# Layer 1's experts in pairs of tiles from tile 13 on, with larger portions in the late edge blocks

## The chip, the core and the metric

The kernel runs on one core of one Trainium2 chip. The metric is the device time of one execution in microseconds; times of several executions are given by their median. The engines are named as the profile names them: PE is the matrix engine, PEld its weight loads, DVE the vector engine, ACT the scalar engine, POOL the engine that issues the indirect gathers, SP the engine whose queue issues most plain transfers.

## The reference, cut to what matters

The program is a two-layer graph network on 3125 nodes of 256 values and 100000 edges, sorted by destination. Layer 0 (two mean-aggregation steps, a linear attention, a mixture of 8 experts) is untouched. The change is in layer 1, which computes

```python
xn = _layernorm(x, axis=-1)
x = x + _L1_gnn_ref(xn, ...) + _L1_mix_ref(xn[None], ...)[0]
x = x + _L1_ffn_ref(_layernorm(x, axis=-1)[None], ...)[0]
...
h1 = relu(einsum('bsd,edh->bseh', features, expert_w1) + expert_b1)
h2 = relu(einsum('bseh,ehf->bsef', h1, expert_w2) + expert_b2)
expert_out = einsum('bsef,efo->bseo', h2, expert_w3) + expert_b3
```

`_L1_gnn_ref` is a graph attention over the edges (a softmax over the edges of each destination, then a weighted sum of source rows). `_L1_ffn_ref` computes all six experts of three 256x256 layers for every node, and mixes the best two by a router. A node's experts can start only when all its incoming edges have been summed.

## The kernel before, in words

The nodes lie in 25 tiles of 128 (`NB = 25`), and the running sum of layer 1 is `xs[:, t, :]`. Layer 1 is the class `Layer1`, and the order of its instructions on PE, DVE and ACT is written out by hand (`manual_schedule`): what an engine gets first it runs first.

**Edge blocks.** The edges are cut into `NK = 31` blocks: block 0, blocks 1 to 29 of 28 columns of 128 edges, and the small block 30. `run` walks over them. For block b it first issues the gathers of block b+1 (`gather`, L1592: one indirect transfer per column on POOL, into the tiles `r0`, 16 columns, with three buffers, and `r1`, 12 columns, with two), and then calls `block(b)`, which on PE, DVE and ACT computes scores, a running maximum, exponentials, the messages (L1700, DVE) and their sums by destination (L1706, PE, tile `sums`). The sums of block b-1 are divided and placed into `xs` inside block b (`close`, `place` L1762, `placed` L1770). When the last block that touches a node tile has been placed, the tile is closed: `settle`, `deviation`, `normed` and `turned` (L1813, L1815) normalise it and put its transpose into the tile `xt`. At most one tile is closed in a block, except in the last `LASTS = 4` blocks, 27 to 30, where `whole` places the block's own sums at once and closes all that is ready.

**Expert groups.** `TOGETHER` lists which neighbouring tiles share one pass of the experts, as (first tile, number of tiles). When `turned` has transposed the last tile of a group, it appends `group(t0, nt, xt)` to `self.queue`. `group` is a generator. Between its `yield`s it issues units: one expert layer half (`layer`, L1447: four matmuls over all the group's columns, 256 for a pair and 384 for three tiles, then an activation, L1450), a result for up to two tiles (`result`, L1516: eight matmuls; its addition into `xs`, L1522, is held back in `self.late`), the router (L1439, L1462 and a chain of small DVE operations, L1464 to L1505), and a bias step (L1533 to L1541). It also issues the weight loads on SP (`weights`, 256 KB each, 18 per group, tile names `ew1` to `ew3` with two buffers each, L358). At most one group runs at a time.

**The planner.** Each `yield` names the unit's cost in the planner's own units, called credits here: `1.8 * nt / 4` for a layer half, 0.9 per tile for a result. `take(x)` adds x to `self.credit` and issues units until the credit is used up; when no group is queued the credit is set to zero, and the place stays empty. `block` calls `take` at eleven places: four before the exponentials with 2, 2, 1 and 2 credits, and seven between the message pieces that share 12; so a block takes 19 credits, times `PORTION.get(b, 1.0)`. `whole` takes 2 + 2 more, and 1 + 1 for each tile it closes. What is left after the last block is issued by `take(1e9)`.

**Other queues around it.** `places(b+2)`, at the end of block b, issues four loads `a<-apart` (L1349) on SP, behind any weight load that still waits for its buffer; their consumer is the matmul L1388 of the next block. `store` issues finished output tiles on SP.

The lines that the change touches are these constants:

```python
942  GB = 3
943  TOGETHER = [(0, 2), (2, 2), (4, 3), (7, 3), (10, 3), (13, 3), (16, 2), (18, 2), (20, 2), (22, 1), (23, 2)]
944  LASTS = 4
945  PORTION = {NK - 6: 1.2, NK - 5: 1.2, NK - 4: 1.2, NK - 3: 1.2, NK - 2: 1.0, NK - 1: 0.5}
```

and the lines that use them:

```python
1605         more = PORTION.get(b, 1.0)
1606         takes = [x * more for x in (2, 2, 1, 2, 12, 0)] if self.keyed else KEYING
...
1807         t0, nt = next(g for g in TOGETHER if g[0] <= b < g[0] + g[1])
```

(in line 1807, b is the tile that is being closed.)

Of the kernel before, what the change touches and what calls it, by code (L numbers as in the profile page):

```python
# [915 lines left out]
NK = len(BQ)  # L916
# [23 lines left out]
WHOLE = [[t for t in range(NB) if max(b for b in range(NK) if t in TILES[b]) == k] for k in range(NK)]  # L940
CW = QC
GB = 3
TOGETHER = [(0, 2), (2, 2), (4, 3), (7, 3), (10, 3), (13, 3), (16, 2), (18, 2), (20, 2), (22, 1), (23, 2)]
LASTS = 4
PORTION = {NK - 6: 1.2, NK - 5: 1.2, NK - 4: 1.2, NK - 3: 1.2, NK - 2: 1.0, NK - 1: 0.5}
KEYING = (3.2, 3.2, 0, 3.2, 0, 1.6)
GROUPS1 = GROUPS[:5] + [(2560, 256), (2816, 256), (3072, 128)]
TS = 256
# [356 lines left out]
class Layer1:  # L1305
# [293 lines left out]
    def block(self, b, part, A, N):  # L1599
# [4 lines left out]
        mk, m4 = A["mk"], A["m4"]  # L1604
        more = PORTION.get(b, 1.0)
        takes = [x * more for x in (2, 2, 1, 2, 12, 0)] if self.keyed else KEYING
# [195 lines left out]
    def turned(self):  # L1802
# [3 lines left out]
        nc = self.nc  # L1806
        t0, nt = next(g for g in TOGETHER if g[0] <= b < g[0] + g[1])
        g = b - t0
# [1178 lines left out]
```

## Time and profile before

| what | value |
|---|---|
| four runs | 3466.73, 3452.87, 3470.64, 3467.14 us |
| their median | 3466.94 us |
| the profiled execution's own time | 3462.25 us |
| its span, first to last instruction | 3460.2 us |
| mean granted clock of PE | 0.812 |
| PE busy | 2360.6 us (68%), 11819 matmuls |
| DVE busy | 1682.6 us (49%) |
| ACT busy | 896.8 us (26%) |
| POOL busy | 1039.3 us (30%) |
| gathers `r` on POOL | 826, 949 ns each at the median, from 1637.6 to 3300.8 us |

Layer 1's edge blocks begin at 1720.7 us, when DVE adds the first scores, and run to the end. A block's start is read here from DVE's first score operation of the block (L1636). A busy share says how long an engine had an instruction in hand; what a stage costs is read from the waits inside it. The granted clock is the share of PE's full clock that the profiler records. An idle time that the profile puts down to "remote" or to "another core or an unknown queue" is one whose releaser it could not name; this program has only one core.

### The profile page before, as it was taken

How to read it: one execution, taken by the hardware profiler on the slowest of the kernel's cores; microseconds unless marked ns; L12 is line 12 of the kernel's file. 1: busy time of each engine (PE TensorE's matmuls, PEld its weight loads, DVE VectorE, ACT ScalarE, POOL GpSimd, SP SyncE). 2: the span in 40 equal slices, each digit the busy share in tenths (PEclk: the TensorE clock that was granted, in tenths of full speed). 3: DMA queues.
4: the chain of work that ended last, by engine and by line, in shares of the span. 5: the costliest groups of instructions: out<-in, count | busy, mean ns of one | idle time of the engine just before them, and what ended most of it. 6: DMA issues, size and time to landing. Idle time of an engine off the chain costs nothing.

```text
span 3460.2 us, 35973 instructions
## 1 busy us (share of the span) xinstructions
PE 2360.6 (68%) x11819; PEld 1614.5 (47%) x11819; DVE 1682.6 (49%) x4292; ACT 896.8 (26%) x1978; POOL 1039.3 (30%) x1075
## 2 busy tenths in 40 slices
PE   2888899998666999798253535455465756555667
PEld 1555577777455888344242323233232323224445
DVE  6887665676300212532053645455545556444553
ACT  2444334554111232222021211122122212112223
POOL 1000000022354000500625354535545455463310
PEclk9999999996777999899575656677677778777889
DMA  3222477442434667444423233434434444343433
GB/s 116 64 66 64 137 263 244 121 129 69 153 114 132 215 212 245 138 161 159 115 72 90 79 87 103 117 110 128 129 106 133 115 120 128 98 132 101 129 96 99
DMA packets 432701, 440.24 MB, mean 127 GB/s; under 512 B 167736, under 2 KB 376678, under 8 KB 432372
## 3 DMA queue, kind: packets, MB, share of 16 engines
q1 hardware_dynamic: 336750, 268.60, 25.5%
q0 software_dynamic: 50128, 130.98, 13.5%
q10 hardware_dynamic: 45622, 38.21, 3.8%
q8 instruction: 98, 1.61, 0.2%
q14 instruction: 103, 0.84, 0.1%
HBM read 337.43 MB, written 100.22 MB: 126 GB/s over the span
## 4 chain that ended last, share of the span: by engine, by line
PE 19%; another core or an unknown queue 16%; DVE 11%; issue 9%; ACT 2%; DMA 1%; DVEq 0%; SPq 0%; ACTq 0%; POOL 0%
PE hp L1447 6%; PE hp L2905 5%; PE yp L1516 3%; PE sums L1706 2%; DVE r L1700 2%; DVE own L1399 1%; DVE tm L1636 1%; PE yp L1845 1%; PE hp L1439 1%; PE yp L1539 1%; DVE ot L1378 1%; DVE lf L1637 1%; DVE ad L1401 1%; ACT h L1450 0%
## 5 line engine op out<-in xcount | busy, mean ns | idle before, releaser
L1592 POOL DMA_INDIRECT r<-tab,b_at x826 | 804.4, 974 | 1019.5 <-PE dp L1388 250.7
L2751 PE MATMUL agg<-wide,px 128*128 128x512 f32 (+5 forms) x1500 | 372.1, 397 | 7.8 <-issue 6.8
L2751 PEld LDWEIGHTS agg<-wide,px 128*128 128x128 f32 (+1 forms) x1500 | 272.0, 206 | 63.1 <-issue 14.8
L2358 POOL DMA_INDIRECT route_x<-x,slot x50 | 52.4, 1049 | 752.2 <-DVE route_at L2353 651.6
L2574 PE MATMUL fhp<-fxe,fw 128*128 128x256 f32 (+1 forms) x992 | 222.8, 381 | 80.5 <-issue 42.5
L1700 DVE TENSOR_TENSOR r<-r,fixed 128x1024 f32<-128x1024 f32 x207 | 247.5, 1209 | 55.7 <-ACT fixed L1679 54.2
L1706 PE MATMUL sums<-r,oh 128*32 128x264 f32 x1652 | 190.1, 483 | 113.5 <-issue 60.0
L1516 PE MATMUL yp<-ew,h 128*128 128x256 f32 x600 | 170.3, 431 | 141.9 <-DVE xs L1770 115.6
L1450 ACT ACTIVATE h<-hp,bc 128x256 f32<-128x256 f32 (+2 forms) x264 | 131.6, 502 | 432.2 <-PE hp L1447 209.3
L2574 PEld LDWEIGHTS fhp<-fxe,fw 128*128 128x128 f32 x992 | 178.4, 206 | 123.4 <-ACT fhid L2575 48.5
L1447 PE MATMUL hp<-h,ew 128*128 128x256 f32 (+2 forms) x528 | 178.2, 469 | 49.5 <-issue 28.0
L1516 PEld LDWEIGHTS yp<-ew,h 128*128 128x128 f32 x600 | 122.5, 214 | 175.5 <-DVE xs L1770 122.0
L2905 PE MATMUL hp<-wt,xt 128*128 128x512 f32 x400 | 185.8, 618 | 19.3 <-ACT xt L351 9.8
L2575 ACT ACTIVATE fhid<-fhp,fb 128x256 f32<-128x256 f32 (+1 forms) x248 | 109.5, 446 | 343.0 <-PE fhp L2574 199.7
L2582 PE MATMUL fyp<-fw,fhid 128*128 128x256 f32 x864 | 191.6, 379 | 0.0
L1447 PE MATMUL hp<-xt,ew 128*128 128x256 f32 (+2 forms) x528 | 177.7, 465 | 10.1 <-issue 7.1
L2582 PEld LDWEIGHTS fyp<-fw,fhid 128*128 128x128 f32 x864 | 161.9, 190 | 20.8
L1522 DVE SCALAR_TENSOR_TENSOR xs<-yp,wgt,xs 128x256 f32<-128x256 f32 x150 | 66.3, 475 | 180.1 <-PE yp L1516 103.6
L1706 PEld LDWEIGHTS sums<-r,oh 128*32 128x32 f32 x1652 | 46.4, 119 | 229.4 <-issue 132.3
L1447 PEld LDWEIGHTS hp<-h,ew 128*128 128x128 f32 x528 | 103.3, 212 | 98.4 <-issue 43.4
L2871 POOL DMA_INDIRECT y<-route_y,slot x50 | 48.7, 974 | 332.9 <-DVE kv_mean L1300 301.2
L2746 ACT CAST wide<-at 128x512 fp32r<-128x512 bf16 (+5 forms) x190 | 101.6, 541 | 162.2 <-PE agg L2751 132.0
(525 smaller groups left out, 3933.6 us busy)
## 6 DMA issues: line engine op xcount, KB each, us to landing
fw<-in_L_ffn_W SPq DMA_DIRECT2D x62, 1024.0 KB
ew<-in_L_ffn_expert_w SPq DMA_DIRECT2D x198, 256.0 KB
at<-adj SPq DMA_DIRECT2D x44, 640.0 KB
route_x<-zero SPq DMA_DIRECT2D x104, 256.0 KB
tab<-stage SPq DMA_DIRECT2D x25, 1056.0 KB
oe<-b_order ACTq DMA_DIRECT2D x117, 168.0 KB
adj<-adj_o SPq DMA_DIRECT2D x78, 250.0 KB
r<-tab,b_at POOLq DMA_INDIRECT x826
```

What stands on the lines that cost most here:

```text
L1447: nc.tensor.matmul(hp[:, :W], ws[i, e][:, n, j * P:(j + 1) * P], x[:, n, :W], start=(n == 0), stop=(n == 1))
L1450: nc.scalar.activation(o[:, j, :W], hp[:, :W], AF.Relu, bias=b[:, e, j:j + 1])
L1516: nc.tensor.matmul(y[:, i - i0, :], h2[e][:, n, i * P:(i + 1) * P], ws[3, e][:, n, :], start=(n == 0), stop=(n == 1))
L1592: st = self.nc.gpsimd.indirect_dma_start(out=r[:, q, c, :], out_offset=None, in_=self.table, in_offset=bass.IndirectOffsetOnAxis(ap=self.B ...
L1700: nc.vector.tensor_tensor(rv, rv, x[:, :, :, None].to_broadcast([P, n, HD, DH]), OP.mult)
L1706: mm = nc.tensor.matmul(self.sums[q * QD:(q + 1) * QD, :], ohs[j][:, q, c, :], r[:, q, c, :], start=(s0 + c == 0), stop=(s0 + c == QC - 1))
L2574: nc.tensor.matmul(hp, w1[:, k, i * P:(i + 1) * P], xe[:, k, :], start=(k == 0), stop=(k == 1))
L2575: nc.scalar.activation(hid[:, i, :], hp, AF.Gelu, bias=b1[:, 0, i:i + 1])
L2582: nc.tensor.matmul(yp, hid[:, i, t * P:(t + 1) * P], w2[:, i, :], start=(i == 0), stop=(i == K1 - 1))
L2746: nc.scalar.copy(wide[:n, :cw], at[:n, i, :cw])
L2751: nc.tensor.matmul(agg[g][:, :cw], px[:n, j, k, g * P:(g + 1) * P], wide[:n, :cw], start=(k == 0 and j == 0), stop=(k == NB - 1 and j == 1))
L2905: nc.tensor.matmul(hp.rearrange("p r d -> p (r d)"), xt[:, k, :], wt[:, k, j * 512:(j + 1) * 512], start=(k == 0), stop=(k == 1))
```

## The change

Two constants change. `TOGETHER` keeps the groups up to tile 12; from tile 13 on, its groups of 3, 2, 2, 2, 1 and 2 tiles become six pairs. `PORTION` becomes 1.3 for blocks 19 to 29, where it was 1.0 for blocks 19 to 24, 1.2 for 25 to 28 and 1.0 for 29; the last block keeps 0.5.

```diff
-TOGETHER = [(0, 2), (2, 2), (4, 3), (7, 3), (10, 3), (13, 3), (16, 2), (18, 2), (20, 2), (22, 1), (23, 2)]
+TOGETHER = [(0, 2), (2, 2), (4, 3), (7, 3), (10, 3), (13, 2), (15, 2), (17, 2), (19, 2), (21, 2), (23, 2)]
 LASTS = 4
-PORTION = {NK - 6: 1.2, NK - 5: 1.2, NK - 4: 1.2, NK - 3: 1.2, NK - 2: 1.0, NK - 1: 0.5}
+PORTION = {**{b: 1.3 for b in range(19, NK - 1)}, NK - 1: 0.5}
```

There are 11 groups before and after, so the number of weight loads stays 198. No other line changes.

## Prediction

> **What bounds the kernel now.** I read the page first, then the chain of waits, then PE's timeline in a late block, then one window per edge block. On the page no engine is full (PE 68%, DVE 49%), and in the chain that ended last
>
> ```profile
> PE 19%; another core or an unknown queue 16%; DVE 11%; issue 9%; ACT 2%; DMA 1%; DVEq 0%; SPq 0%; ACTq 0%; POOL 0%
> ```
>
> 16% are waits without a named releaser. PE's timeline shows what stands there (start, duration, instructions, idle time before them):
>
> ```profile
> 3090.33 0.37 PE L1388 MATMUL dp<-a,ot 96*128 96x64 bf16 x7
> 3090.53 1.11 PE L1762 MATMUL yp<-y,to 128*128 128x256 f32 x4
> 3120.14 2.08 PE L1516 MATMUL yp<-ew,h 128*128 128x256 f32 x4 [28.50 <-DVE xs L1770]
> ```
>
> PE stands for 28.5 us, and DVE's L1770 waits for these four L1762 matmuls. POOL's timeline has this block's 28 gathers from 3080.5 to 3115.7, their last packets land near 3117, and PE goes on at 3120. It is so in every block: PE works for 10 to 30 us after the first gather, then stops or crawls until the gathers' end. In the crawl its records step by 1.40 us, a weight load or a matmul at a time, so a matmul by 2.8:
>
> ```profile
> 1696.28 0.21 PE L1388 MATMUL dp<-a,ot 96*128 96x64 bf16 x1 [2.59 <-issue]
> 1699.08 0.21 PE L1388 MATMUL dp<-a,ot 96*128 96x64 bf16 x1 [2.59 <-issue]
> ```
>
> Why, the trace does not say. But a block has thus two parts: about 37 us of gathers, with only so much PE work in them, and after them whatever PE work is left. Windows of the two parts, for blocks 21 and 25 (stretch, length, then PE, PEld, DVE, ACT and POOL busy with counts, clock, DMA share, GB/s):
>
> ```profile
> 2861.90:2898.90 37.00, 19.82 (x79) 10.91 (x78) 15.03 (x36) 7.86 (x17) 27.25 (x28) 0.84 0.53 149
> 2898.90:2915.80 16.90, 15.47 (x81) 6.98 (x81) 11.81 (x19) 2.59 (x5) 0.00 (x0) 0.74 0.13 30
> ...
> 3080.50:3117.10 36.60, 9.26 (x50) 6.34 (x46) 10.32 (x28) 4.08 (x9) 26.88 (x28) 0.70 0.55 156
> 3117.10:3150.20 33.10, 25.88 (x142) 16.73 (x143) 22.01 (x55) 10.41 (x23) 0.00 (x1) 0.81 0.22 68
> ```
>
> Both lose 37 us to the gathers; block 25 then has 142 matmuls left, against 81, and takes 33.1 us for them, against 16.9. So **a block costs the gathers and the expert work that falls behind them**. One window per block, from start to start (same columns):
>
> ```profile
> 2400.40:2446.90 46.50, 23.99 (x130) 11.68 (x128) 26.33 (x54) 8.00 (x19) 28.44 (x30) 0.71 0.44 115
> ...
> 2761.00:2806.90 45.90, 25.23 (x152) 14.01 (x151) 26.58 (x56) 11.09 (x23) 27.42 (x28) 0.81 0.48 136
> 2806.90:2862.70 55.80, 32.16 (x160) 17.22 (x159) 30.22 (x76) 10.89 (x27) 26.92 (x29) 0.72 0.41 116
> 2862.70:2917.60 54.90, 36.30 (x164) 18.33 (x163) 27.80 (x58) 10.88 (x24) 27.89 (x30) 0.81 0.41 115
> ...
> 3082.30:3151.10 68.80, 34.23 (x191) 22.76 (x190) 31.43 (x81) 14.04 (x32) 26.30 (x28) 0.75 0.39 110
> 3151.10:3213.40 62.30, 37.11 (x202) 25.78 (x201) 28.78 (x59) 11.65 (x29) 26.50 (x29) 0.75 0.44 129
> 3213.40:3285.20 71.80, 41.89 (x229) 29.83 (x230) 33.58 (x89) 17.35 (x42) 31.80 (x34) 0.76 0.42 118
> 3285.20:3355.30 70.10, 44.16 (x222) 29.95 (x220) 31.82 (x83) 16.19 (x38) 12.61 (x14) 0.76 0.34 102
> 3355.30:3394.00 38.70, 33.46 (x213) 24.26 (x211) 25.31 (x69) 15.32 (x42) 0.00 (x0) 0.96 0.43 129
> 3394.00:3460.20 66.20, 49.49 (x204) 37.80 (x204) 19.52 (x66) 19.51 (x45) 0.00 (x0) 0.90 0.28 82
> ```
>
> These are blocks 12, 19, 20, 21 and 25 to 30. Blocks 9, 22, 23 and 24 take 59.0, 54.0, 56.6 and 54.1 us.
>
> **The change, part by part.** *What is issued* hardly changes: 11 groups, 198 weight loads, the same columns in all. A layer half of a triple (1.45 us of PE in the timeline) and of a single (0.61) cost 2.06 us, of two pairs (1.03 each) 2.06. I cost this at 0; its bound is one group's 25 layer halves by 0.1 us, 2.5 us either way.
>
> *Where it is issued* changes. I walk through `take` with each unit's credits and the blocks in which tiles close (13 in block 17, 15 in 20, 17 in 22, 19 in 25, 21 in 27, 23 in 29, 24 in 30). Credits before and after:
>
> | block | 19 | 20 | 21 | 22 | 23 | 24 | 25 | 26 | 27 | 28 | 29 | 30 |
> |---|---|---|---|---|---|---|---|---|---|---|---|---|
> | before | 15.45 | 18.9 | 18.9 | 15.45 | 18.9 | 18.9 | 22.9 | 22.5 | 29.2 | 29.2 | 24.5 | 4.05 |
> | after | 18.15 | 24.3 | 24.7 | 24.3 | 14.8 | 24.3 | 11.2 | 24.3 | 17.5 | 19.8 | 31.0 | 4.5 |
>
> Both rows sum to 238.85, and the last pair, 35.5 credits, is issued behind block 30 in both: **the tail is the same**, and work only moves between blocks. After the change, places stay empty in blocks 19, 23, 25 and 27 (up to the third message piece) and at the end of 28.
>
> *The price of a credit.* PE alone: the last pair runs from 3410.6 to 3453.4 us, 42.8/35.5 = 1.2 us a credit with its waits, 1.0 in its dense part (a layer half 1.03 us, 0.9 credits). Blocks of triples: 18.9 credits took 54.8 us (mean of blocks 14, 15, 17, 18, 20, 21, 23, 24), blocks 12 and 13, with 9.0 and 7.35, took 46.5 and 45.5: (54.8 - 46.0)/(18.9 - 8.2) = **0.82 a credit**. Blocks of pairs: 9.0 credits 46.5 us (block 12); 18.9 took 59.0 and 62.0 (blocks 9, 11); 22.9 and 22.5 took 68.8 and 62.3: (65.6 - 46.5)/(22.7 - 9.0) = **1.39 a credit**. A pair's credit holds 4.4 matmuls, a triple's 3, and by the crawl above fewer of a pair's columns get through beside the gathers.
>
> *Blocks 19 to 26*, from the nearest row: 19: its pattern took 51.3, 45.9 and 54.0 (blocks 16, 19, 22), mean 50.4, + 2.7 x 0.82 = 52.6. 20 and 21: 55.8 + 5.4 and 54.9 + 5.8 credits at 1.0 = 61 each. 22, a pair with its router inside the gathers as in block 25: pairs' line, 46.5 + 1.39 x 15.3 = 67.8. 23 and 25 on the same line: 54.6 and 49.6. 24 and 26, without the router's chain, as block 26: 62.3 + 1.8 x 1.0 = 64 each. Sum 474.6; before 452.4: **+22**. Bounds: the triples' line for all pairs (59.2 at 24.3 credits) and block 19 at its own 45.9 + 2.2: 446, -7; block 25's price (70) for each pair of 24.3, 1.39 for 20 and 21, and block 16's 51.3 and more (54.2) for 19: 494, +42.
>
> *Blocks 27 to 30.* 27: 71.8 less 11.7 credits, at 1.0 to 1.39: 55.5 to 60.1, I take 58. 28: 70.1 less 9.4 credits, 57 to 60.7, plus `whole`'s chain, which has no unit beside it now (in block 30 the same chain runs from the placing at 3406.5 to the router's matmul at 3410.6, with 3 us of sums ahead): about 5, I take 64. 29: no gathers, clock 0.96: 38.7 + 6.5 x 1.2 = 46.5. 30: + 0.5. Sum 235.2, before 246.8: **-11.6**; bounds -22 (1.39 a credit and no bare chain) and -5.
>
> *Queues.* `places` and the weight loads keep their order on SP. Where places are empty, a group's first five loads are issued only when it starts; its first matmuls need 256 KB tiles that land behind the gathers or beside the 0.13 to 0.2 of DMA share after them, within the 2 to 5 us above. The nearest row, the last pair, has 3 us from its transposes (3409.5) to its first layer half (3412.5), so I add nothing.
>
> **Sum:** +22 - 11.6 = +10 against the profiled execution's 3462.25 us: 3472. The median of the four runs lies 4.7 above that execution, so 3471 against it is a change of +0.1%, and of +0.3% against the execution itself. 0.5% (17 us) is about what a measurement of this kernel can tell from no change.
>
> **The clock.** After the 28.5 us stand, four L1516 matmuls took 2.08 us; in the dense tail they take 1.03, and block 29, without gathers, has a clock of 0.96. So an empty place can make the next matmuls dear. [...] But the gathers' stand halves the clock in every block already, so the sum above goes without it.
>
> **Rivals.**
> *Slower: pairs at block 25's price.* Blocks 22, 24 and 26 carry 24.3 credits in pairs. If PE, stepping through narrower matmuls beside the gathers, hides as little as in block 25 (50 matmuls of 192), each costs 68.8 + 1.4 x 1.0 = 70, together 14 more than I sum (2 + 6 + 6); with 1.39 for 20 and 21, 5 more: 3490. For: blocks 9, 11 and 25. Against: block 26. It decides once these three average over 67 us.
> *Faster: the late relief wins.* Blocks 25 to 28 took 273 us, 53.8 more than four of 54.8 for 28.2 credits more, 1.9 us a credit. If 24.3 credits cost the triples' 0.82, because the larger portions ahead of the first sums lie beside the gathers for nothing, blocks 19 to 26 end near 450 us, -2, and 27 to 30 near their bound, -20: 3440. For: block 21 hid 79 matmuls beside the gathers. Against: block 27, with 1.2 portions, hid 45.
> *No effect.* Equal credits, equal tail, a straight price per credit: 3464.
>
> **How the numbers follow.** Forecast 3471: 0.35 (of it 0.03 past 0.5%); slower rival 0.29; faster 0.24; no effect 0.12. So within 0.5% 0.44, slower 0.32, faster 0.24. The bounds give 3462 - 7 - 22 = 3433 and 3462 + 42 - 5 = 3499; I give 3433 to 3500, which leaves out little of any case.
>
> **What would show it.** Blocks 22, 24, 26 at 62 to 68 us, 23 and 25 near 50 to 55, 28 below 66, 29 longer by 6 to 8, 30 unchanged. Wrong, if pair blocks of 24.3 credits take under 60 us or over 70, if the stand beside the gathers changes its length, or if block 30 moves.

## The result, and the profile after

The changed kernel took 3474.62 us (median of 52 runs) against 3466.94 of the kernel before (78 runs): a ratio of 1.0026, interval 1.0015 to 1.0036. The profiled execution took 3479.59 us with a span of 3477.5.

What the whole profile shows has not moved: PE 2367.4 us busy (2360.6 before), again 11819 matmuls and 198 weight loads. The chain that ended last, by engine, from the page of the changed kernel:

```profile
PE 20%; another core or an unknown queue 16%; DVE 11%; issue 9%; ACT 2%; DMA 1%; POOL 0%; ACTq 0%; DVEq 0%; SPq 0%; POOLq 0%
```

The 16% without a named releaser are still there, and so is the crawl of 2.8 us a matmul. From PE's timeline of the changed kernel (start, duration, instructions, idle time before them):

```profile
1696.27 0.21 PE L1388 MATMUL dp<-a,ot 96*128 96x64 bf16 x1 [2.59 <-issue]
1699.07 0.21 PE L1388 MATMUL dp<-a,ot 96*128 96x64 bf16 x1 [2.59 <-issue]
```

So what changed is where the expert work lies. One window per edge block of the changed kernel, blocks 19, 20, 22 to 26 and 28 to 30 (stretch, length, then PE, PEld, DVE, ACT and POOL busy with counts, clock, DMA share, GB/s):

```profile
2762.00:2825.80 63.80, 30.53 (x160) 16.47 (x158) 28.17 (x65) 12.55 (x25) 26.21 (x28) 0.71 0.36 103
2825.80:2886.30 60.50, 41.60 (x180) 22.80 (x180) 30.02 (x70) 11.67 (x29) 26.84 (x29) 0.77 0.42 115
...
2942.20:3012.30 70.10, 39.19 (x204) 26.81 (x203) 31.14 (x77) 13.28 (x34) 27.63 (x30) 0.76 0.41 118
3012.30:3075.50 63.20, 29.40 (x157) 17.84 (x156) 29.96 (x78) 12.22 (x27) 25.85 (x28) 0.63 0.39 113
3075.50:3138.40 62.90, 40.36 (x209) 28.02 (x207) 28.09 (x57) 12.31 (x30) 27.73 (x29) 0.75 0.44 125
3138.40:3191.40 53.00, 28.26 (x142) 16.23 (x141) 28.97 (x74) 11.82 (x26) 27.73 (x29) 0.62 0.42 115
3191.40:3255.50 64.10, 38.51 (x210) 27.68 (x208) 28.67 (x59) 12.54 (x30) 27.29 (x29) 0.75 0.44 128
...
3316.70:3366.80 50.10, 30.54 (x172) 21.57 (x172) 28.39 (x58) 11.49 (x26) 12.28 (x13) 0.76 0.36 106
3366.80:3412.20 45.40, 42.07 (x204) 30.08 (x203) 24.69 (x65) 16.68 (x39) 0.00 (x0) 0.89 0.24 73
3412.20:3477.50 65.30, 49.49 (x200) 37.42 (x199) 19.75 (x67) 18.94 (x43) 0.00 (x0) 0.91 0.27 83
```

Blocks 21 and 27 take 55.9 and 61.2 us. Blocks 19 to 26 together took 452.5 us before and 493.5 after, **+41**; blocks 27 to 30 took 246.8 and 222.0, **-24.8**. Blocks 0 to 18, whose code is the same, took 12 us more in this execution and began 11 earlier. Net, the two profiled executions differ by 17.3 us, the medians by 7.7: one execution lay under its median and the other above. Sums of blocks from single profiles carry a spread of that size: blocks 0 to 18 took 1040 to 1053 us in the five profiles of this pair and of set 1 below that leave the gathers as they are, and 1025 to 1030 in three of set 3.

The dearest surprise is block 19. It has 2.7 credits more than before and took 17.8 us more. The two parts of blocks 19 and 25 of the changed kernel (gathers, then what is left):

```profile
2762.00:2799.00 37.00, 7.52 (x39) 5.26 (x37) 8.62 (x23) 5.77 (x12) 25.20 (x27) 0.69 0.49 143
2799.00:2825.80 26.80, 23.01 (x121) 11.21 (x121) 19.55 (x42) 6.78 (x13) 1.01 (x1) 0.73 0.17 47
3138.40:3175.00 36.60, 14.52 (x66) 8.02 (x64) 18.55 (x37) 6.31 (x14) 26.08 (x27) 0.58 0.47 129
3175.00:3191.40 16.40, 13.74 (x76) 8.21 (x77) 10.42 (x37) 5.52 (x12) 1.65 (x2) 0.71 0.30 85
```

Of block 19's 160 matmuls 39 ran beside the gathers and 121 were left; of block 25's 142, 66 and 76. PE's timeline of block 19 in the changed kernel shows the same picture as block 25 of the kernel before:

```profile
2770.09 0.37 PE L1388 MATMUL dp<-a,ot 96*128 96x64 bf16 x7
2770.30 1.11 PE L1762 MATMUL yp<-y,to 128*128 128x256 f32 x4
2800.52 2.07 PE L1516 MATMUL yp<-ew,h 128*128 128x256 f32 x4 [29.11 <-DVE xs L1770]
```

The first gather is at 2760.3 and the stand begins 11 us later, at the four placing matmuls, and lasts 29 us. In block 19 of the kernel before, 12 of the old group's last 24 result matmuls (L1516) are still to come behind the placing, where the changed kernel has 4 left. PE goes on there after 1.8 us, and stands only later, for 14.5 us, when the old group has ended:

```profile
2767.18 1.13 PE L1762 MATMUL yp<-y,to 128*128 128x256 f32 x4 [0.41 <-issue]
2770.09 2.86 PE L1516 MATMUL yp<-ew,h 128*128 128x256 f32 x12 [1.78 <-DVE xs L1770]
...
2791.27 2.93 PE L1439 MATMUL hp<-xt,rw 128*128 128x384 f32 x4 [14.49 <-issue]
```

### The profile page after: what moved, and what is told of

Read it like the earlier page. It is cut to its first block, busy times and chain, and to the rows that moved or that the text cites. A ratio compares the mean times of both kernels' runs of the same rounds, so it can differ in the third digit from the quotient of the medians.

```text
span 3477.5 us, 35968 instructions
## 1 busy us (share of the span) xinstructions
PE 2367.4 (68%) x11819; PEld 1628.9 (47%) x11819; DVE 1682.3 (48%) x4291; ACT 899.1 (26%) x1979; POOL 1033.4 (30%) x1075
## 3 DMA queue, kind: packets, MB, share of 16 engines
q0 software_dynamic: 50128, 130.98, 13.5%
## 4 chain that ended last, share of the span: by engine, by line
PE 20%; another core or an unknown queue 16%; DVE 11%; issue 9%; ACT 2%; DMA 1%; POOL 0%; ACTq 0%; DVEq 0%; SPq 0%; POOLq 0%
PE hp L1447 6%; PE hp L2905 5%; PE yp L1516 3%; PE sums L1706 2%; DVE r L1700 2%; DVE own L1399 1%; PE hp L1439 1%; ACT h L1450 1%; DVE ot L1378 1%; DVE ad L1401 1%; PE yp L1956 1%; DVE tm L1636 0%; PE yp L1845 0%; DVE xs L1522 0%
## 5 line engine op out<-in xcount | busy, mean ns | idle before, releaser
L1516 PE MATMUL yp<-ew,h 128*128 128x256 f32 x600 | 169.6, 432 | 158.3 <-DVE xs L1770 137.1
L2358 POOL DMA_INDIRECT route_x<-x,slot x50 | 52.3, 1047 | 751.0 <-DVE route_at L2353 652.8
L2574 PE MATMUL fhp<-fxe,fw 128*128 128x256 f32 (+1 forms) x992 | 226.9, 385 | 68.4 <-ACT fhid L2575 50.1
L1450 ACT ACTIVATE h<-hp,bc 128x256 f32<-128x256 f32 (+1 forms) x264 | 131.3, 501 | 506.9 <-PE hp L1447 234.8
L1706 PE MATMUL sums<-r,oh 128*32 128x264 f32 x1652 | 182.9, 490 | 112.4 <-DVE r L1700 77.6
L1516 PEld LDWEIGHTS yp<-ew,h 128*128 128x128 f32 x600 | 125.0, 217 | 190.2 <-DVE xs L1770 143.1
L1447 PE MATMUL hp<-h,ew 128*128 128x256 f32 (+1 forms) x528 | 180.3, 474 | 44.2 <-ACT h L1450 27.8
L1447 PE MATMUL hp<-xt,ew 128*128 128x256 f32 (+1 forms) x528 | 188.6, 490 | 29.8 <-ACT h L1450 17.7
L2905 PE MATMUL hp<-wt,xt 128*128 128x512 f32 x400 | 187.6, 623 | 17.3 <-issue 10.5
L1447 PEld LDWEIGHTS hp<-xt,ew 128*128 128x128 f32 x528 | 114.8, 229 | 81.4 <-ACT h L1450 29.2
L1770 DVE TENSOR_TENSOR xs<-xs,yp 128x512 f32<-128x512 f32 (+1 forms) x35 | 22.3, 641 | 261.6 <-remote 249.7
L2871 POOL DMA_INDIRECT y<-route_y,slot x50 | 48.1, 963 | 330.9 <-DVE kv_mean L1300 298.5
```

Of the source, the lines that this page charges most:

```text
L1447: nc.tensor.matmul(hp[:, :W], ws[i, e][:, n, j * P:(j + 1) * P], x[:, n, :W], start=(n == 0), stop=(n == 1))
L1450: nc.scalar.activation(o[:, j, :W], hp[:, :W], AF.Relu, bias=b[:, e, j:j + 1])
L1516: nc.tensor.matmul(y[:, i - i0, :], h2[e][:, n, i * P:(i + 1) * P], ws[3, e][:, n, :], start=(n == 0), stop=(n == 1))
L1706: mm = nc.tensor.matmul(self.sums[q * QD:(q + 1) * QD, :], ohs[j][:, q, c, :], r[:, q, c, :], start=(s0 + c == 0), stop=(s0 + c == QC - 1))
L2358: st = nc.gpsimd.indirect_dma_start(out=self.x, out_offset=bass.IndirectOffsetOnAxis(ap=self.slot[:n, i, t:t + 1], axis=0), in_=x2[:n, t - ...
L2574: nc.tensor.matmul(hp, w1[:, k, i * P:(i + 1) * P], xe[:, k, :], start=(k == 0), stop=(k == 1))
```

## The experiments

**Theory: bunching.** Pairs cost nothing of their own. The larger portions use a group up before the next is there; a filled block then stands beside an emptied one, and the emptied one gives little back, because PE stands until the gathers end whatever is queued behind. **Rivals:** pairs are dear beside the gathers (1.39 us a credit instead of 0.82); or nothing but chance moves.

The runs came in four sets, each on one chip with runs of the kernel before on that chip. The chips proved to be of two kinds: the kernel before took 3469.2 us in the first set, 2708.7 in the second, 3414.3 in the third and 2705.7 in the fourth. Each chip was met in one set only, so these runs cannot tell the chip from the occasion; "a chip with stands" below means a chip as it was in its set.

### Set 1 (before: 3469.2 us)

**Pairs alone.**

```diff
-TOGETHER = [..., (13, 3), (16, 2), (18, 2), (20, 2), (22, 1), (23, 2)]
+TOGETHER = [..., (13, 2), (15, 2), (17, 2), (19, 2), (21, 2), (23, 2)]
 PORTION = {NK - 6: 1.2, NK - 5: 1.2, NK - 4: 1.2, NK - 3: 1.2, NK - 2: 1.0, NK - 1: 0.5}
```

> The kernel before with the new grouping (pairs from tile 13 on) and the old portions. Walked through the planner, the credits of blocks 19 to 30 are 15.45, 18.9, 18.9, 19.3, 18.9, 19.3, 22.5, 23.8, 25.6, 20.7, 25.6, 9.9: nearly even, with few empty places. My theory: the groups' width is nearly free, and the loss of the change comes from bunching (the larger portions use a pair up before the next is there, and the block left nearly empty still costs 62 us because PE stands there until the gathers end). Then this one loses nothing: 3458 to 3472, blocks 20 to 24 at 54 to 58 us each, and 28 near 56. Rival: pairs themselves are dear beside the gathers (1.39 us a credit instead of 0.82): then blocks 20 to 24 take 60 to 62 us each, about 5 to 6 more each, and the time is 3485 to 3500. No effect of anything: within 0.15% of before.

Measured 3466.79 us, ratio 0.9999 (0.9969 to 1.0029). Its windows of blocks 22, 23 and 28:

```profile
2926.70:2981.20 54.50, 32.00 (x178) 20.65 (x177) 30.63 (x80) 13.68 (x30) 27.55 (x28) 0.75 0.46 126
2981.20:3036.60 55.40, 32.26 (x182) 21.20 (x180) 27.41 (x56) 11.27 (x28) 28.68 (x30) 0.78 0.48 139
...
3295.90:3347.20 51.30, 30.95 (x176) 21.46 (x176) 28.47 (x58) 11.77 (x27) 11.36 (x12) 0.79 0.36 105
```

With 19.3 and 18.9 credits, blocks 22 (which begins with the rest of a triple) and 23 (all pairs) take 55 us each, as triples did. Blocks 20 to 23 are all at 54 to 56.5 (20 and 21 run the triple of tile 10 in both kernels); only 24 (63.8) is above the expected 58, and 28 is 5 below. Blocks 19 to 26 are 12 above the kernel before, 27 to 30 are 13.5 below. That pairs are dear falls for the whole kernel.

**Portions alone.**

```diff
 TOGETHER = [..., (13, 3), (16, 2), (18, 2), (20, 2), (22, 1), (23, 2)]
-PORTION = {NK - 6: 1.2, NK - 5: 1.2, NK - 4: 1.2, NK - 3: 1.2, NK - 2: 1.0, NK - 1: 0.5}
+PORTION = {**{b: 1.3 for b in range(19, NK - 1)}, NK - 1: 0.5}
```

> The kernel before with the old grouping (triple at tile 13, single at 22) and the new portions (1.3 for blocks 19 to 29). Credits of blocks 19 to 30 by the planner: 18.15, 24.3, 18.9, 10.05, 24.3, 24.7, 24.3, 14.8, 26.1, 31.0, 22.25, 0. Blocks 22 and 26 are left nearly empty and block 30 has no unit. My theory (bunching costs): the emptied blocks 22 and 26 give back less than 1 us a credit (they stay at 50 us and 56 us or more), the filled ones 20, 23, 24 pay 5 to 6 each: 3475 to 3490. Rival (pairs are dear, portions are not): no loss, 3455 to 3470.

Measured 3480.85 us, ratio 1.0038 (1.0008 to 1.0068): inside the theory's range, outside the rival's. Block 19 took 63.6 us, as in the changed kernel. Of the emptied blocks, 22 (10.05 credits) took 49.9 and 26 (14.8 credits) 64.7; the filled 23 (24.3) took 66.3. Not every filled block pays: 24 (24.7 credits) took 55.2, against 54.1 with 18.9 before.

**A single as the last group.**

```diff
-TOGETHER = [..., (20, 2), (22, 1), (23, 2)]
+TOGETHER = [..., (20, 2), (22, 2), (24, 1)]
-PORTION = {..., NK - 1: 0.5}
+PORTION = {..., NK - 1: 2.0}
```

> The kernel before with its last two groups exchanged, (22,2),(24,1) for (22,1),(23,2), and a portion of 2.0 in the last block. Behind block 30 then stands a single, 17.75 credits instead of 35.5. By the tail's 1.2 us a credit that is 21 us less behind block 30, and the 17.75 credits go into block 30, where PE would stand beside chains of small operations: 10.8 credits less are issued in block 29 (places empty until 23 is closed) and 31 more in 30. My theory (a credit costs about 1.1 us wherever no gather runs, as in 29 and 30, and the sum is the same): gain only from chains that lie beside PE work in block 30, 0 to 10 us: 3457 to 3467. Rival (the tail is bound by PE alone, and a single is dearer by column than a pair): slower, 3467 to 3480.

Measured 3483.72 us, ratio 1.0044 (1.0021 to 1.0067): the theory's range missed, the rival's upper end passed by 4 us. Blocks 29 and 30 of this version:

```profile
3360.80:3385.50 24.70, 17.42 (x108) 10.29 (x106) 20.87 (x43) 7.02 (x16) 0.00 (x0) 0.90 0.24 74
3385.50:3476.90 91.40, 71.01 (x310) 56.25 (x309) 24.48 (x92) 27.98 (x70) 0.00 (x0) 0.82 0.31 94
```

Block 29 gave back 14.0 us for 13.7 credits (10.8, which the expectation gives as the difference, is what is left in it), but block 30 with the tail grew by 25.2. The closing single ran from 3439.5 to the span's end at 3476.9, store included; from its first to its last matmul (3470.6) that is 31 us for 17.75 credits, 1.75 a credit. The closing pair of the kernel before took 1.2. A group's chain is not shorter for one tile: PE's waits for the router, the bias step and `ew` sum to 5.3 us in the single's timeline, and to 3.4 in that of the closing pair.

**Plain transfers instead of indirect ones, blocks 20 to 29.** The computation leaves out the choice of rows by source. The run asks what PE's stand belongs to.

```diff
+                    if b >= 20:
+                        st = self.nc.gpsimd.dma_start(out=r[:, q, c, :], in_=self.table[i % 150 * P:(i % 150 + 1) * P, :])
+                    else:
                         st = self.nc.gpsimd.indirect_dma_start(
...
```

> The kernel before, whose indirect gathers in blocks 20 to 29 are replaced by plain transfers of the same size issued by POOL from fixed rows of the same table: the computation leaves out the choice of rows by source, so the messages are those of other nodes; instructions on PE, DVE and ACT are unchanged. [...] If it belongs to the bytes that land in SBUF beside PE's reads, the stand stays as long as 28 transfers of 64 KB take, or it comes earlier. If it belongs to something in the schedule (a wait of L1762 on something else), the blocks stay within 2 us of 54 to 70 us.

Measured 3207.73 us in one run, 261 under the kernel before. Blocks 0 to 17, still indirect, keep their times (54.2 us in block 15, 51.4 in 16, against 54.0 and 51.3); blocks 19 to 26 fall from 452.5 to 264.0 us. Block 25, which took 68.8:

```profile
2931.60:2972.20 40.60, 32.53 (x191) 21.01 (x190) 31.31 (x80) 13.99 (x32) 14.09 (x28) 0.92 0.61 188
```

The same 191 matmuls, the same DVE work, as many bytes; PE is busy for 32.5 of 40.6 us. So on this chip the stand comes with the indirect transfers, and 28 us of block 25 were that. Whether it is their indirection or their length on POOL (0.97 us against 0.55) this run does not tell. Block 18, in which POOL issues 12 indirect gathers and then 16 plain transfers, took 38.2 us against 54.5 in the kernel before, with no wait of PE over 4.1 us: 12 indirect gathers in a row did not make a stand there.

### Set 2 (before: 2708.7 us)

**The changed kernel with block 19's portion put back.**

```diff
-PORTION = {**{b: 1.3 for b in range(19, NK - 1)}, NK - 1: 0.5}
+PORTION = {**{b: 1.3 for b in range(20, NK - 1)}, NK - 1: 0.5}
```

> The changed kernel with one size put back: block 19 has portion 1.0 again, the larger portions begin at block 20. Credits of blocks 19 to 30: 15.45, 24.3, 24.7, 25.2, 16.6, 24.3, 11.2, 24.3, 17.5, 19.8, 31.0, 4.5 (2.7 credits go from block 19 to 22 and 23, nothing else). Block 19 took 45.9 to 53.8 us with portion 1.0 (three kernels), and 63.8 and 63.6 with 1.3 (the changed kernel and the portions alone). If it is the portion that makes PE stand 29 us early in block 19 (its expert units are used up ahead of the sums' placing, and PE has nothing but the placing in hand), block 19 comes back to 46 to 54, 22 and 23 grow by 1 to 2 us each, and the time is 3460 to 3468. Rival: block 19's 63.7 is chance in where the stand falls, or the triple-to-pair boundary; then 19 stays above 60 and the time stays within 3 us of 3474.6.

Measured 2699.56 us, ratio 0.9967 (0.9953 to 0.9981), on a chip where the expectation had no ground to stand on: the stands are missing. The page's chain has no unknown releaser any more:

```profile
PE 18%; POOL 12%; DVE 10%; issue 6%; DMA 3%; ACT 2%; DVEq 0%; SPq 0%; ACTq 0%; POOLq 0%
```

POOL has taken its place: blocks 12 to 18 last 35 to 37 us each, which is 28 gathers at 1.25 us. A block there comes out near the longer of its gathers and PE's work, or somewhat above both (block 22: 46.1 us, with POOL busy for 35.1 and PE for 39.5).

**One pause in the gathers** (kernel before; the second part of a block's gathers waits for the placed sums):

```diff
+            if j and b >= 2:
+                self.rest = fetch
+            else:
+                fetch()
...
         self.placed()
+        self.fetch_rest(self.xs[:, TILES[b - 1][0], 0:1])
```

> The kernel before with its 28 gathers per block in two parts: the 16 columns of r0 at the block's start as now, the 12 of r1 only when DVE has added the placed sums of the block before into xs (a one-column copy on POOL waits for that); blocks 1 to 28. If PE's stand is a matter of how long POOL's indirect transfers run without a pause (it began 10 to 30 us after the first gather in every block), then 16 gathers (20 us) leave a shorter stand, the second part meets a PE that has caught up, and a block of 55 us falls to 43 to 50: 3250 to 3400. If it is only that PE gets little done while they run, wherever they lie, the blocks get longer by the pause and by messages that come late: 3480 to 3650.

Measured 2717.84 us, ratio 1.0037 (1.0022 to 1.0053); without stands this could not tell the two apart.

**The changed kernel with plain transfers** (blocks 20 to 29; the choice of rows left out, the diff as in set 1).

> The changed kernel with the indirect gathers of blocks 20 to 29 replaced by plain transfers from fixed rows of the same table, as in the run of the kernel before with plain transfers (3207.7 us): the choice of rows by source is left out. If the change moves work only, and what it lost in blocks 19 to 26 was PE's stand beside the gathers, then without the stand the blocks 20 to 28 cost what PE's own work costs, the emptied ones become short in proportion (1.0 to 1.2 us a credit), and the whole stays within 8 us of 3208 apart from block 19, whose stand is in blocks with plain gathers too only by its first part. If pairs or bunching cost PE time of their own, it is 3220 to 3240.

Measured 2697.02 us in one run, against 2708.7 of the kernel before there; not comparable with 3208. Its blocks 19 to 30 sum to 482.1 us, those of the indirect version with block 19 put back to 481.7. On this chip indirect or plain makes no difference to the late blocks.

### Set 3 (before: 3414.3 us, with the stands)

**The changed kernel again.** No edit.

> The changed kernel itself, unedited. Two kinds of chip have shown: one on which the kernel before takes 3467 to 3469 us with PE standing in every gather, and one on which it takes 2709 us without the stands, a block then costing some 36 us of gathers or PE's work, whichever is longer. On the first kind: 1.001 to 1.004 of before, 3472 to 3481. On the second, my theory (bunching costs only where PE stands beside the gathers) says that filled blocks of 24 credits there pay 34 to 46 us while emptied ones fall to 36, and that the late relief of blocks 27 and 28 counts in full: 2697 to 2703, about 0.997 of before, as the version with block 19 put back. Rival (the loss is in the schedule itself, on any chip): 1.002 to 1.004 of before there too, 2714 to 2720.

Measured 3440.40 us, ratio 1.0083 (1.0052 to 1.0115): the same sign, three times the size, above the expected 1.004. Block 19 took 61.1 us, 22 again 70.1.

**Block 19's portion put back**, now where it tells something:

> The changed kernel with block 19's portion at 1.0 again. Its first run fell on a chip without the stands and said nothing on the question it was made for. On a chip with the stands: if the portion is what made block 19 stand 29 us early, block 19 is 46 to 54 us and the time 3460 to 3468 (8 to 14 under the changed kernel); if chance or the triple-to-pair boundary, block 19 stays above 60 and the two are within 3 us. On a chip without: within 2 us of the changed kernel by my theory, since block 19 there costs 32 to 36 either way.

Measured 3431.95 us, ratio 1.0047 (1.0021 to 1.0073), 8.5 under the changed kernel on the same chip; the difference foretold was 8 to 14. The two intervals overlap, so this difference of the medians alone is not clear of noise; the block's own time is plainer. Block 19 took 45.4 us against 61.1. Block 22 fell to 63.8 from 70.1 and 23 rose to 66.3 from 59.5. One size, 2.7 credits, moved three blocks by 6 to 16 us each.

This kernel is the one of set 2, so the two chips can be laid side by side. Block 23 on the chip with stands, from PE's timeline:

```profile
2970.94 0.37 PE L1388 MATMUL dp<-a,ot 96*128 96x64 bf16 x7
2971.15 1.11 PE L1762 MATMUL yp<-y,to 128*128 128x256 f32 x4
3003.84 1.11 PE L1706 MATMUL sums<-r,oh 128*32 128x264 f32 x8 [31.58 <-DVE r L1700]
```

and on the chip without:

```profile
2386.88 0.37 PE L1388 MATMUL dp<-a,ot 96*128 96x64 bf16 x7
2387.08 1.11 PE L1762 MATMUL yp<-y,to 128*128 128x256 f32 x4
2390.72 0.65 PE L1706 MATMUL sums<-r,oh 128*32 128x264 f32 x8 [2.53 <-DVE r L1700]
```

The same instructions, 31.6 us of standing against 2.5. The block takes 66.3 us on the one chip and 38.7 on the other.

**One pause again.**

> The kernel before with the gathers of each block in two parts, the second behind DVE's adding of the placed sums; its first run fell on a chip without the stands (2717.8 against 2708.7). On a chip with them: if the stand is a matter of how long POOL's indirect transfers run without a pause, 3250 to 3400; if PE only gets little done while they run, wherever they lie, 3480 to 3650. On a chip without the stands: 1.002 to 1.005 of before again, since the gathers there are the longer side of a block and the pause lengthens them.

Measured 3524.70 us, ratio 1.0338 (1.0283 to 1.0392): the second reading. But the test was weaker than meant. POOL's timeline of this version:

```profile
2759.46 0.98 POOL L1593 DMA_INDIRECT r<-tab,b_at  x1 [0.56 <-ACT fixed L1690]
...
2793.32 0.95 POOL L1593 DMA_INDIRECT r<-tab,b_at  x1 [0.30 <-issue]
2814.24 0.18 POOL L1606 COPY pause<-xs 128x1 f32<-128x1 f32 x1 [19.98 <-DVE xs L1782]
```

The second part of one block ran straight into the first part of the next: still 28 gathers in one run of 35 us, only elsewhere in the block.

**Portions alone again.**

> The kernel before with the new portions alone. On a chip with the stands 1.001 to 1.007 of before, as in its first run (1.0038). On a chip without them: my theory (no cost of bunching beside gathers that PE can work through) says that its 24-credit blocks pay about what they save later, but block 30 gets no unit and 28 gets 31 credits: 2700 to 2712. Rival (bunching is dear on any chip): 2714 to 2725.

Measured 3441.57 us, ratio 1.0095 (1.0062 to 1.0128): a little above the expected 1.007, and the same as the changed kernel there (1.0083). The portions carry the loss, with triples as with pairs. Block 19 took 54.9 us here: the stand at the same place lasted 12.3 us, and a second one of 9.5 us followed. Blocks 19 to 26 took 460.3 us, 20 less than in the profile of the same kernel in set 1. The kernel before was not profiled on this chip, so in which blocks the loss of set 3 lies is not shown.

### Set 4 (before: 2705.7 us)

**Four short runs of gathers** (kernel before; the gathers of a block released in parts of 8, 8, 6 and 6 by DVE's progress):

```diff
+        self.fetch_rest(raw[:, 0:1], 8)
...
+            self.fetch_rest(self.y[:, 0, 0:1], 8)
...
+            self.fetch_rest(self.xs[:, TILES[b - 1][0], 0:1], 6)
...
+                self.fetch_rest(part[j][2][:, 0, lo, 0:1], 28)
```

> The kernel before with the gathers of a block in four short runs, 8, 8, 6 and 6, each released by DVE's progress in the block that runs beside them (first scores, the division of the sums, the placed sums, the third message piece; a one-column copy on POOL waits for each); blocks 1 to 28. In the version with one pause the second part of a block ran on without a break into the next block's first part, so that POOL's unbroken runs were again near 35 us, and PE crawled or stood from 12 to 18 us after their start to their end. Theory: the stand needs an unbroken run of over some 10 us; then runs of 7.5 to 10 us leave PE nearly free, and on a chip with the stands a block falls from 55 to 40 to 48 us: 3050 to 3300. Rival: PE gets its few instructions per gather however they lie, and each pause adds to the block: 3550 to 3750. On a chip without the stands the gathers are the longer side of a block and the pauses lengthen it: 1.01 to 1.10 of before.

Measured 2782.08 us, ratio 1.0285 (1.0268 to 1.0302), on a chip without stands: the pauses lengthen the blocks there, as said (from 1700 to 2600 us POOL's copies wait 49.7 us for DVE). Whether short runs of gathers would free PE on a chip with stands **stays open**; no run of it fell on one. Two stretches of other traces bear on it: block 18 of the plain transfers in set 1, and layer 0 (last section).

The blocks in one table (us, from the windows; the two kinds of chip are not to be compared with each other):

| block | before | after | pairs alone | portions alone | after, set 3 | portions alone, set 3 | from 20, set 3 | from 20, set 2 |
|---|---|---|---|---|---|---|---|---|
| 19 | 46.0 | 63.8 | 53.8 | 63.6 | 61.1 | 54.9 | 45.4 | 31.9 |
| 22 | 54.0 | 70.1 | 54.5 | 49.9 | 70.1 | 48.7 | 63.8 | 46.1 |
| 23 | 56.5 | 63.2 | 55.4 | 66.3 | 59.5 | 59.2 | 66.3 | 38.7 |
| 28 | 70.0 | 50.1 | 51.3 | 61.0 | 50.3 | 57.1 | 49.5 | 31.2 |
| 19 to 26 | 452.5 | 493.5 | 464.6 | 480.2 | 486.3 | 460.3 | 472.6 | 301.4 |
| 27 to 30 | 246.8 | 222.0 | 233.3 | 245.3 | 220.3 | 238.7 | 219.1 | 180.3 |

## Why the prediction was right, and where it was not

Forecast 3471, measured 3474.6; 1.0026 lies within 0.5%. The frame held on chips with stands: nothing but the places changed, and a block is its gathers and what falls behind them. The sum came out so near because two errors offset each other, and that part of the agreement is luck. It also mixed two baselines: the +10 is added to the profiled execution (3462) and read against the median of the runs (3467); added to the median it gives 3477. Measured were +7.7 between the medians and +17.3 between the profiled executions.

Shown by the runs: the portions by themselves lose as much as the whole change (1.0038 beside 1.0026, and 1.0095 beside 1.0083 in set 3), and in block 19 the larger portion moves the stand to the placing. The pairs by themselves show no loss, though their interval reaches 1.0029. That the rest of the loss comes from filled blocks beside emptied ones is read from rows of single profiles; no run tests it by itself.

- *What is issued:* unchanged, as said.
- *Blocks 20 to 22 and 24 to 26:* 60.5, 55.9, 70.1, 62.9, 53.0 and 64.1 us against 61, 61, 67.8, 64, 49.6 and 64: each within 5.1, the sum within 1. Of the signs that were named, 22 (70.1) and 23 (63.2) lie outside theirs, 22 just above the 70 that was to show it wrong; 24 to 26, 28, 29 and 30 came as said. (The list of blocks in which tiles close names the last block that touches a tile; in the trace, L1813 turns tile 13 in block 20 and tile 15 in 22. The credits of the table are right all the same: the groups start where it has them.)
- *The emptied places, blocks 19 and 23:* the term that was mis-sized. 52.6 and 54.6 were forecast, 63.8 and 63.2 measured, 20 us together, almost all of the +41 beyond the +22. I priced them by credits on a straight line. What happens is another stand: the old group's units are used up ahead of the placing matmuls (in block 19 all but four matmuls), and PE stands from there, 11 to 12 us after the first gather, for 27 to 29 us. In block 19 this goes with the portion in all eight profiles from chips with stands that leave the gathers as they are: with 1.3 PE stands at the placing for 29.1, 29.2, 28.3 and 12.3 us, and the block takes 54.9 to 63.8; with 1.0 it waits there for 1.7 to 3.3 us, stands later for 9.6 to 20.2, and the block takes 45.4 to 53.8. Putting 19's portion back in set 3 took 15.7 us off that block. An emptied block with 14.8 credits is no cheaper than a full one: 63.2 (23; 59.5 in set 3), and 64.7 for block 26 of portions alone (61.3 in set 3). One with 10 to 11 is: 53.0 and 49.9. Why PE stands in block 19 already at the placing, and in block 25 of the same run (a wait of 2.5 us there) does not, is not settled.
- *Block 28:* 64 forecast, 50.1 measured. I added 5 us for `whole`'s bare chain; but from the placing to the next block's first score took 8 us before, with 6 credits in it, and 6 after, so the 70.1 held that chain already. And 9.4 credits fewer are 50 matmuls and 13.6 us of PE here, with the router's waits gone besides (the group starts a block earlier). The pairs alone show the same (51.3), and on a chip without stands the same fall (31.2, against 53.3 with the schedule of before in the paused version).
- *Blocks 27, 29, 30:* 61.2, 45.4, 65.3 against 58, 46.5, 66.7. The tail is the same, as said.
- *Rivals:* "pairs at block 25's price" needed an average over 67 in blocks 22, 24 and 26; it was 65.7, and the pairs alone cost nothing. "The late relief wins" was right for blocks 27 to 30 and wrong for 19 to 26 on this chip; on a chip without stands the nearest version, block 19 put back, was 0.9967. There the late blocks give back 21.5 us against the paused version, which has the schedule of before, and blocks 19 to 26 cost only 10. "No effect" falls: 1.0083 in set 3.
- *The clock:* the sum has no price of its own for dearer matmuls behind empty places, and the total (3474.6 against 3471) does not decide whether one was due. The rows show low clocks in emptied blocks on both kinds of chip: 0.62 in block 25 of the changed kernel, and 0.69 without stands, between neighbours at 0.98; but there the block lasts 37.2 us, about its 28 gathers, so no cost of the low clock shows there.

The number thus holds for the kind of chip that the profile of before came from. I had taken the stand for a property of the kernel; the same kernel runs without it on other chips, and there the sign of the change is probably the other. The unedited changed kernel was not run there, and neither was the profile of the kernel before.

No version that computes the same result ran faster than both kernels on a chip with stands; the pairs alone equal the kernel before.

## What to carry to other kernels

Price work that is moved between stages by the row of the stage that it makes, an emptied one too: a stage with a fixed wait need not get shorter by what is taken out of it (14.8 credits cost what 18.9 did, or more; 10 to 11 cost less), so filling one and emptying its neighbour can cost twice (24.3 and 14.8 credits in neighbouring blocks took 124 to 134 us in four profiles, two blocks of 18.9 about 110). Split a change into its parts before explaining it: here one part cost nothing that could be measured and the other as much as the whole. And where a large wait has no named releaser, run the kernel before on more than one chip before building on it.

## What the runs showed of the hardware that was not expected

- The same kernel takes 3467, 3469 or 3414 us on some chips and 2709 or 2706 on others, over 700 us less, with the same work: PE 2251 us busy in the version profiled there. PE stands or steps at 1.40 us per instruction in the one case while POOL's indirect gathers run, and not in the other.
- The whole difference lies beside runs of indirect transfers on POOL. The kernel with block 19's portion put back was profiled on both kinds of chip, and its 11819 matmuls, in the same order in both traces, can be laid side by side. Up to 906 us the two differ by 3.2 us at most. From 906 to 1085 us POOL issues 118 indirect transfers (L1151) in runs of 15, some 18 us each, with breaks of 1 to 18 us, and the last 28 in one: the chip with stands falls back by 95 us (517 matmuls fill its time from 900 to 1100 us, 514 that of the other from 900 to 1004). From 1100 to 1390, without such transfers, the distance stays 96.2 us; from 1394 to 1469 50 more of them (L2871) make it 110; up to 1630 it stays; beside the gathers it grows to 718; behind them it grows by only 6 more.
- Short runs far apart cost nothing there: from 692 to 826 us POOL issues 40 indirect transfers (L2358) in runs of 8, some 10 us each, with breaks of 20 to 21 us. PE, busy for 85% of 690 to 875 us, keeps within 3.2 us of the other chip. Other work runs beside them than in the edge blocks, so this only suggests that short runs would help there.
- On a chip with stands, plain transfers of the same bytes on POOL do away with it (261 us over ten blocks); on one without, they change nothing in the late blocks (482.1 against 481.7 us).
- What PE waits for is open. The timed executions agree with the profiled ones (medians of 3474.62 and 3466.94 us, after and before, against 3479.59 and 3462.25); each comes with its span and clock, so none is known to have run without recording, and no run here shows whether recording has a part in the stand.
